# Attention keys on another DMA queue: stacks loaded in thirds, from a copy in DRAM that lies as in SBUF

## The chip, the cores and the metric

The kernel runs on one core of a Trainium2 chip. The metric is the device time of one execution in microseconds (us), as the median of several runs. A core has five engines that run side by side and wait for one another by semaphores: TensorE (PE, matrix products; PEld is its loading of weights), VectorE (DVE), ScalarE (ACT), GpSimd (POOL) and SyncE (SP), which here does nothing but issue DMAs. ScalarE can issue DMAs too; they then stand on a queue of its own, and among ScalarE's own instructions. SBUF is the core's memory with 128 partitions, PSUM the memory that TensorE writes, DRAM the large memory outside.

## What is computed

Four images of 384 channels and 48 x 48 = 2304 pixels pass through one attention layer with 8 heads of 48 channels. The queries get a depthwise 7 x 7 convolution of the image added.

```python
local = conv_general_dilated(x, conv_w, padding='SAME', feature_group_count=C)   # 7 x 7
local_flat = batch_norm(local).reshape(B, C, N).transpose(0, 2, 1)
x_norm = _layernorm(x_flat, ln_gamma, ln_beta)
q, k, v = (x_norm @ qkv_w.T + qkv_b)          # 8 heads of 48, N = 2304 pixels
q = q + _layernorm(local_flat, ln_gamma, ln_beta)
attn = softmax(einsum('bhnd,bhmd->bhnm', q, k) * scale)
out = einsum('bhnm,bhmd->bhnd', attn, v)
out = x_flat + (out @ proj_w.T + proj_b)
```

(The batch norm is written short here.) All tensors are float32.

## The kernel before

**Tiling.** An image's 2304 pixels are cut into NG = 6 groups of G = 384. There are NT = 24 groups over the four images, counted by t; b is the image and g the group in it. The 8 heads are worked in NP = 4 pairs. The keys' pixels are cut into KB = 18 blocks of 128.

**The attention of one group.** The loop from L1063 goes through NSLOT = 12 slots: 4 pairs, each in three thirds of BATCH = 6 key blocks. One slot is `score_batch` (L879) and `weigh_batch` (L884). `score` makes, for one key block, six matmuls of the stacked keys `ks` with the stacked queries `qs` (L856) into a PSUM tile `r`, and ScalarE takes the exponential of it (L864) into `pt`. `weigh_batch` multiplies the six `pt` of a slot with the values (L871) into a PSUM tile `o`, which ScalarE copies out (`sums_out`, L756 and L766) and VectorE adds up (`sums_add`, L775). Tiles `r` and `o` come from one pool of four buffers of two banks each.

**Stacks.** Scores are made at full float32 accuracy out of high and low parts. `key` (L570) splits the keys into a high part (L575, ScalarE) and a low part (L576, VectorE) in one tile `k` of 128 partitions x 2 x 384. `keys_out` (L519) writes `k` to the DRAM tensor `keys[b]`, head by head: four DMAs for each of the three tiles `k` of a group, since heads 6 and 7 are spread over all three. `stack_keys` (L533) then puts together the stack of a pair in SBUF: `stacks[b, p]`, 128 partitions x 2 x 2304, with high and low parts of two heads in the order that the six matmuls want. That takes eight DMAs: per head one of 48 partitions, one of 16 and two of 32. Two buffers hold stacks. For the first pair of an image's first group the stack is made piece by piece, a group's keys at a time; for all other pairs it is loaded whole, in the first third of the pair before (L1066 to L1070), so 23 whole stacks an image, each from `keys[b]`. Queries are stacked alike: `high_queries` (L725) casts on ScalarE (L728), `low_queries` (L730) subtracts on VectorE (L733) and then issues six DMAs (four for the last pair) that move rows of the tile within SBUF (L738, L740).

**Other small DMAs.** `sums_add` sends the softmax denominators `den` to DRAM (L780), and after the last pair moves rows of the outputs (`ao`, L784). `divide` (L788) loads them again as `rd` (L794), inverts them on VectorE (L795), writes them (`rden`, L799) and spreads them over partitions (`rb`, L804 and L807). The layer norms' sums go over DRAM as `parts` and `four` (L460, L461), and `few_in` reads `four` on VectorE (L470). `gather_tails` (L509) collects the fourth pair's queries in `qt` (L513) after `query_end` (L714). `load_slab` brings image rows for the convolution, `load_x` the next image's x (both L94), `hold` and `fetch` outputs that wait for their projection.

**The rest.** Between images the loop from L1009 makes keys, values and queries of the next image, and projects the last image's outputs. The convolution (L288) is 147 VectorE operations a group; a planner (`plan`, L358) spreads them over the slots. In the groups whose `coming` is true, the next image's x is loaded and normalised as well: the last two groups of the first image and the last three of the second and third.

**Order.** Instructions on TensorE, VectorE and ScalarE stand as the program writes them (`manual_schedule`, L84). All DMAs named so far are SyncE's, and their order on SyncE is the framework's. A DMA waits at issue for its data, for its buffer, and for one of eight completion semaphores that the framework gives out in turn.

Of the kernel before, what the change touches and what calls it, by code (L numbers as in the profile page):

```python
# [10 lines left out]
F32 = mybir.dt.float32  # L11
HALF = mybir.dt.float32r
# [4 lines left out]
P = 128  # L17
NH = 8
HD = 48
# [5 lines left out]
BATCH = 6  # L25
# [20 lines left out]
def unshifted_pass(  # L46
# [16 lines left out]
    nc = tc.nc  # L63
    B, C, N = x.shape
# [3 lines left out]
    G = RG * W  # L68
    NG = N // G
    NB = G // P  # L70
    NP = NH // 2
# [7 lines left out]
    big = ctx.enter_context(tc.tile_pool(name="big", bufs=1))  # L79
    work = ctx.enter_context(tc.tile_pool(name="work", bufs=2))  # L80
    dram = ctx.enter_context(tc.tile_pool(name="dram", bufs=2, space=bass.MemoryType.DRAM))
# [4 lines left out]
    def two_banks(name="r"):  # L86
        return ps.tile([P, 2, 512], F32, tag="r", name=name)
# [15 lines left out]
    def load_x(b, g):  # L103
        load_packed(place_x(b, g), x[b, :, g * G : (g + 1) * G])
# [79 lines left out]
    for c in range(CC):  # L184
        for r, n, first in ((0, HD, 0), (64, HD, 1), (48, 16, 6), (112, 16, 7)):
            head = first + 2 * c if first < 6 else first
            ch = head * HD + (16 * c if first >= 6 else 0)
            while n:
                part = min(n, P - ch % P)
                pieces.append((c, r, ch // P, ch % P, part))  # L190
                r, n, ch = r + part, n - part, ch + part
# [141 lines left out]
    def later(b):  # L333

        return X_LATER + (b == 1)
# [33 lines left out]
    def convolve(*point):  # L369
        for _ in range(share[point]):  # L370
            next(stream)
# [145 lines left out]
    keys, values = {}, {}  # L517

    def keys_out(b, g, u, k):  # L519
        at = slice(g * G, (g + 1) * G)  # L520
        for j in range(2):
            r = 64 * j
            for head, rows, n in (
                (2 * u + j, slice(0, HD), (r, r + HD)),
                (6 + j, slice(16 * u, 16 * u + 16), (r + HD, r + 64)),
            ):
                nc.sync.dma_start(
                    out=keys[b][head, rows, :, at], in_=k[n[0] : n[1]].bitcast(F32)
                )

    stacks = {}

    def stack_keys(b, p, at=slice(0, N)):  # L533

        if at.start == 0:
            stacks[b, p] = big.tile([P, 2, N], HALF, tag="ks", name=f"ks{b}_{p}", bufs=2)
        dst = stacks[b, p].bitcast(F32)
        for j in range(2):
            r, head = 64 * j, keys[b][2 * p + j]
            nc.sync.dma_start(out=dst[r : r + HD, 0, at], in_=head[:, 0, at])  # L540
            nc.sync.dma_start(out=dst[r + HD : r + 64, 0, at], in_=head[0:16, 1, at])
            for i in range(2):
                nc.sync.dma_start(
                    out=dst[r + 32 * i : r + 32 * i + 32, 1, at], in_=head[16:HD, 1, at]
                )

    def from_x(b, g, before=None, ao=None):

# [63 lines left out]
    def both(making):  # L612
        next(making)
        next(making)
# [7 lines left out]
    rows = {}  # L622
# [64 lines left out]
    def output_bias():  # L687

        m = two_banks()[:, 0, 0:CC]
        for co in range(CC):  # L690
            project(
                m[:, co : co + 1],
                lambda c: w_o[:, c, co * P : (co + 1) * P],
                lambda c: vbp[:, c, :],
            )
        added = const.tile([P, CC], F32, tag="inv", name="added")
        nc.scalar.copy(added, m)
        return added
# [4 lines left out]
    def local_end(t, rs):  # L703
        acc = accs[t]
        nc.vector.scalar_tensor_tensor(acc, acc, -1.0, rs, ALU.mult, ALU.mult)
# [19 lines left out]
    def high_queries(t, p):  # L725
        qs = work.tile([P, 3, G], HALF, tag="qs", name=f"qs{t}_{p}", bufs=5)
        stacked[t, p] = qs
        nc.scalar.copy(qs[:, 0, :], query_of(t, p))  # L728
# [39 lines left out]
    def sums_add():  # L768

        if not parts_of:  # L770
            return
        t, p, i, part = parts_of.popleft()
        ao, ao3, den = outputs[t]
        dst = (ao[:, p, :] if p < CC else ao3)[0 : 64 + HA]
        nc.vector.tensor_add(dst, dst, part[0 : 64 + HA])  # L775
        if i < KB // BATCH - 1:
            return
        for j in range(2):
            r = 64 * j
            nc.sync.dma_start(out=den[2 * p + j : 2 * p + j + 1], in_=dst[r + HD : r + HA])  # L780
        if p == NP - 1:
            for c in range(CC):
                for r in (0, 64):
                    nc.sync.dma_start(  # L784
                        out=ao[r + HD : r + 64, c, :], in_=ao3[r + 16 * c : r + 16 * c + 16]
                    )
# [25 lines left out]
    def load_residual(t, tag="qs", bufs=5):  # L812
        b, g = divmod(t, NG)
        xr = work.tile([P, CC, G], F32, tag=tag, name=f"xr{t}", bufs=bufs)
        nc.sync.dma_start(
            out=xr, in_=x[b, :, g * G : (g + 1) * G].rearrange("(c p) n -> p c n", p=P)
        )
        residuals[t] = xr
# [81 lines left out]
    def convolve_first(n):  # L900
        nonlocal n_first
        n_first += n
        for _ in range(n):
            next(stream)
# [58 lines left out]
    convolve_first(4)  # L963
    norm.scale(norm.newton())
    both(making)
    stack_keys(0, 0, slice(0, G))
    convolve_first(7)
    for g in range(1, NG):

        last = g == NG - 1  # L970
        making = from_x(0, g)
        both(making)
        assert not last or n_first >= each - PE_TAPS
        norm = Norm(accs[0] if last else xn[0, g + 1])
        norm.sum()
        norm.mean()
        if last:
            added = output_bias()
        convolve_first(4)
        norm.centre()  # L980
        norm.squares()
        both(making)
        if not last:
            convolve_first(4)
            both(making)
        norm.sum_squares()
        norm.mean()
        norm.root()
        if last:
            both(making)  # L990
        both(making)
        convolve_first(6 if last else 10)
        if last:
            local_end(0, norm.newton())
        else:
            norm.scale(norm.newton())
        both(making)
        stack_keys(0, 0, slice(g * G, (g + 1) * G))
        if not last:
            convolve_first(7)  # L1000
    query_end(0)
# [5 lines left out]
    for t in range(NT):  # L1007
        b, g = divmod(t, NG)
        if g == 0 and b:  # L1009

            sums_add()
            load_x(b, NG - 1)
            norms_x = {}
            for gk in range(NG):
                before = t - NG + gk
                load_residual(before)
                making = from_x(b, gk, before, ao if gk < NG - 1 else outputs[before][0])
                new = NG - later(b) + gk if gk < later(b) else None
                old = norms_x.get(gk - 1)
                both(making)  # L1020
                convolve("kv", t, gk, 0)
                if new is not None:
                    norms_x[gk] = Norm(xn[b, new])
                    norms_x[gk].sum()
                    norms_x[gk].out()
                both(making)
                if old:
                    old.few_variance()
                    old.few_root()
                if gk == 1:  # L1030
                    query_end(t)
                    rb = divide(t - 1)
                if gk == 2:
                    last_ao = outputs[t - 1][0]
                    nc.vector.tensor_mul(last_ao, last_ao, rb)
                convolve("kv", t, gk, 1)
                both(making)
                convolve("kv", t, gk, 2)
                if new is not None:
                    norms_x[gk].few_centre()  # L1040
                    norms_x[gk].squares()
                both(making)
                convolve("kv", t, gk, 3)
                if old:
                    old.scale(old.few_newton())
                both(making)
                convolve("kv", t, gk, 4)
                if new is not None:
                    norms_x[gk].sum_squares()
                    norms_x[gk].out()  # L1050
                both(making)
                stack_keys(b, 0, slice(gk * G, (gk + 1) * G))
                if gk == NG - 2:
                    high_queries(t, 0)
                if gk == NG - 1:
                    low_queries(t, 0)
                if gk < NG - 2:
                    ao = fetch(before + 1)
# [4 lines left out]
        for s in range(NSLOT):  # L1063
            score_batch(t, s)
            pair, third = divmod(s, KB // BATCH)
            if third == 0:  # L1066
                if pair < NP - 1:
                    stack_keys(b, pair + 1)
                elif g < NG - 1:
                    stack_keys(b, 0)  # L1070
            if third == 1 and pair < NP - 1:
                high_queries(t, pair + 1)
            if s == 2 and g:
# [71 lines left out]
    for before in range(NT - NG, NT):  # L1145
# [3 lines left out]
        r, r2 = two_banks(), two_banks()  # L1149
# [552 lines left out]
```

## Time and profile before

| | us |
|---|---|
| median of 3 runs | 3101.54 |
| lowest and highest | 3089.67, 3103.32 |
| the profiled execution | 3096.22 |
| its span, first to last instruction | 3094.4 |
| start-up until the first scores | about 190 |
| one group of the attention | 88 to 113 |
| from one image's attention to the next one's | 162 to 175 |

The profile shows one execution. "Busy" is time in which an engine works; a wait is put down to what ended last before the instruction began ("releaser"). "PEclk" is the share of TensorE's full clock that was granted; over the span it was 0.957. DMA issues are not counted as busy, but the timeline shows them, on "SPq" for SyncE and "ACTq" for ScalarE. Over the span the DMA engines moved 401 MB, at a share of 0.64 of their time, nearly all of it from SyncE's queue. In the section on DMA issues the stacks are the three largest entries: 184 DMAs of 432 KB, 368 of 288 KB and 184 of 144 KB.

### The profile page before, as it was taken

The page shows a single profiled execution, that of the slowest core. Times are in us where ns is not written, and L with a number is a line of the kernel's source. Part 1 is how long each engine was busy: PE and PEld are TensorE (multiplying, and loading weights), DVE is VectorE, ACT ScalarE, POOL GpSimd, SP SyncE. Part 2 cuts the span into 40 slices and gives each one's busy share as a digit, 9 for nine tenths or more (in the row PEclk, how much of TensorE's full clock was granted, in tenths as well). Part 3 has the DMA queues.
Part 4 walks back from the last instruction along what each step waited for, and adds up shares of the span by engine and source line. Part 5 has one row for each costly group of instructions (what it writes and reads, how often), then busy time and mean ns, then how long its engine had stood idle before and what let it go on. Part 6 is the DMA issues. An engine that isn't in the chain of part 4 may idle for free.

```text
span 3094.4 us, 52948 instructions
## 1 busy us (share of the span) xinstructions
PE 2846.5 (92%) x19190; PEld 1786.4 (58%) x19190; DVE 2474.7 (80%) x4899; ACT 1655.1 (53%) x2638; POOL 14.9 (0%) x77
## 2 busy tenths in 40 slices
PE   8877898889988999898999899999999989999999
PEld 5445555555555666565655566555555556656665
DVE  7779889888889788786789888878878877888612
ACT  4245555556522666665642366656663246666663
POOL 1000000000000000000000000000000000000000
PEclk9888999999998999999999999999999999999999
DMA  6255666777645767767654677677675557767774
GB/s 135 61 106 97 125 114 126 131 130 132 134 118 144 127 129 134 133 128 137 131 133 129 145 131 137 128 133 134 125 144 129 152 113 138 133 131 143 133 143 157
DMA packets 190926, 401.08 MB, mean 130 GB/s; under 512 B 69504, under 2 KB 150848, under 8 KB 167104
## 3 DMA queue, kind: packets, MB, share of 16 engines
q1 hardware_dynamic: 187120, 393.98, 64.1%
q8 instruction: 154, 2.52, 0.4%
q10 hardware_dynamic: 2992, 3.62, 0.3%
q14 instruction: 116, 0.95, 0.1%
q0 software_dynamic: 544, 0.01, 0.0%
HBM read 307.88 MB, written 55.35 MB: 117 GB/s over the span
## 4 chain that ended last, share of the span: by engine, by line
PE 34%; DVE 33%; DMA 22%; SPq 7%; issue 2%; ACT 1%; POOL 0%; DVEq 0%; ACTq 0%; POOLq 0%
DVE acc L288 21%; PE r L507 13%; PE o L871 11%; PE r L856 10%; DMA ks<-keys 7%; DMA four<-parts 4%; DMA xn<-in_x_dram 3%; DMA parts<-part 3%; SPq L740 3%; DMA qs<-qs 2%; SPq L738 1%; DVE sq L405 1%; DMA rd<-den 1%; DMA rden<-rd 1%; DVE sq L456 1%
## 5 line engine op out<-in xcount | busy, mean ns | idle before, releaser
L288 DVE SCALAR_TENSOR_TENSOR acc<-slab,vec,acc 128x368 f32<-128x368 f32 (+6 forms) x3447 | 1768.5, 587 | 1.2
L864 ACT ACTIVATE pt<-r 128x768 f32<-128x768 f32 x1728 | 1259.7, 827 | 337.6 <-PE r L856 298.9
L856 PE MATMUL r<-qs,ks 64*128 64x384 f32 x10368 | 1092.9, 357 | 201.6 <-DMA qs<-qs 118.3
L856 PEld LDWEIGHTS r<-qs,ks 64*128 64x128 f32 x10368 | 955.3, 196 | 418.7 <-issue 265.9
L871 PE MATMUL o<-pt,v 128*64 128x384 f32 x6912 | 1183.6, 492 | 0.0
L871 PEld LDWEIGHTS o<-pt,v 128*64 128x64 f32 x6912 | 472.8, 137 | 593.0 <-issue 510.6
L507 PE MATMUL r<-xn,w_qk 128*128 128x384 f32 x864 | 293.1, 498 | 0.0
L756 ACT COPY o<-o 113x384 f32<-113x384 f32 x192 | 91.7, 478 | 320.8 <-PE o L871 320.7
L507 PEld LDWEIGHTS r<-xn,w_qk 128*128 128x128 f32 x864 | 169.7, 196 | 120.7 <-issue 11.8
L795 DVE RECIPROCAL rd<-rd 128x24 f32<-128x24 f32 x24 | 7.3, 303 | 189.3 <-DMA rd<-den 189.3
L507 PE MATMUL r<-w_v,xn 128*128 128x384 f32 x432 | 147.0, 493 | 9.7 <-DVE xn L502 8.9
L567 ACT COPY v<-r 128x384 f32<-128x384 f32 x72 | 32.1, 480 | 187.7 <-PE r L507 187.7
L507 PEld LDWEIGHTS r<-w_v,xn 128*128 128x128 f32 x432 | 82.2, 192 | 69.9 <-DVE xn L502 10.5
L470 DVE TENSOR_REDUCE few<-four 128x12 f32<-128x48 f32 x80 | 18.6, 233 | 129.7 <-DMA four<-parts 129.7
L766 ACT COPY ao<-o 113x384 f32<-113x384 f32 x72 | 34.6, 481 | 163.8 <-PE o L871 163.8
L507 PE MATMUL r<-af,w_o 128*128 128x384 f32 x360 | 119.1, 487 | 0.0
L733 DVE TENSOR_TENSOR qs<-xn,qs 128x384 fp32r<-128x384 f32 x72 | 40.0, 556 | 95.9 <-ACT qs L728 95.9
L576 DVE SCALAR_TENSOR_TENSOR k<-r,qkb,k 128x384 fp32r<-128x384 f32 x72 | 44.4, 616 | 67.8 <-ACT k L575 67.4
L507 PEld LDWEIGHTS r<-af,w_o 128*128 128x128 f32 x360 | 68.3, 190 | 47.7 <-issue 0.6
L775 DVE TENSOR_TENSOR ao<-ao,o 113x384 f32<-113x384 f32 x144 | 79.7, 554 | 18.2 <-ACT o L756 18.2
L575 ACT ACTIVATE k<-r,qkb 128x384 fp32r<-128x384 f32 x72 | 41.9, 582 | 92.4 <-PE r L507 43.3
L588 ACT ACTIVATE xn<-r,qkb 128x384 f32<-128x384 f32 x72 | 39.4, 576 | 57.6 <-PE r L507 56.3
(119 smaller groups left out, 906.2 us busy)
## 6 DMA issues: line engine op xcount, KB each, us to landing
ks<-keys SPq DMA_DIRECT2D x368, 288.0 KB
ks<-keys SPq DMA_DIRECT2D x184, 432.0 KB
ks<-keys SPq DMA_DIRECT2D x184, 144.0 KB
qs<-qs SPq DMA_DIRECT2D x528, 48.0 KB
keys<-k SPq DMA_DIRECT2D x144, 144.0 KB
xr<-in_x_dram SPq DMA_DIRECT2D x24, 576.0 KB
slab<-in_x_dram SPq DMA_DIRECT2D x32, 378.0 KB
held<-ao SPq DMA_DIRECT2D x20, 576.0 KB
```

The costliest lines, as they stand in the source:

```text
L288: nc.vector.scalar_tensor_tensor(dst, src, weight, dst, ALU.mult, ALU.add)
L507: nc.tensor.matmul(dst, lhsT=weights(c), rhs=src(c), start=c == 0, stop=c == CC - 1)
L575: nc.scalar.activation(k[:, 0, :], r[:, :G], AF.Identity, bias=bias)
L576: nc.vector.scalar_tensor_tensor(k[:, 1, :], r[:, :G], bias, k[:, 0, :], ALU.add, ALU.subtract)
L588: nc.scalar.activation(src[:, i, :], q[:, :G], AF.Identity, bias=qkb[:, 0, i : i + 1])
L733: nc.vector.tensor_sub(qs[:, 1, :], query_of(t, p), qs[:, 0, :])
L740: nc.sync.dma_start(out=qs[r + 32 * i : r + 32 * i + 32, 2], in_=qs[r + 16 : r + HD, i])
L756: nc.scalar.copy(part[0 : 64 + HA], sums[0 : 64 + HA, 0, :G])
L775: nc.vector.tensor_add(dst, dst, part[0 : 64 + HA])
L856: nc.tensor.matmul(r[:, j, :G], lhsT=ks[rows, w, kb * P : (kb + 1) * P], rhs=qs[rows, m, :], start=i == 0, stop=i == 2,)
L864: nc.scalar.activation(pt, r[:, :, :G], AF.Exp, scale=SCALE)
L871: nc.tensor.matmul(sums[halves[j], 0, :G], lhsT=values[t // NG, kb // NB][:, first : first + 64], rhs=pt[:, j, :], start=i == 0, stop=i == ...
```

## The change

Four things change; the instructions of TensorE, VectorE and GpSimd stay in their order.

- **Whole stacks come on ScalarE's queue.** `stack_keys` goes. `load_keys` (b, p, i) is called in every third of a pair, after the scores of that slot, for the next pair.
- **From a copy, in thirds.** In the second third of each pair of an image's first group, `keep_stack` writes the stack to DRAM as it lies in SBUF (`wide`, 128 x 2 x 2304), in one DMA of 2.36 MB. From the second group on, `load_keys` brings one third of a stack (128 x 2 x 768) in one DMA per slot.
- **In the first group** the copy doesn't exist yet for pairs 1 to 3; these are loaded whole, with eight DMAs from `keys[b]`, on ScalarE's queue. Pair 0 of the second group is already loaded from the copy.
- **The first pair is stacked straight from SBUF.** When `key` has made the first of a group's three tiles (u = 0, which holds heads 0 and 1), `keys_out` issues eight DMAs from it into the stack, and no longer writes these heads to `keys[b]`.

```diff
     def keys_out(b, g, u, k):
         at = slice(g * G, (g + 1) * G)
+        k = k.bitcast(F32)
+        if u == 0:
+            if g == 0:
+                place_keys(b, 0)
+            for j in range(2):
+                stack_head(b, 0, j, k[64 * j : 64 * j + HD], at, nc.sync)
         for j in range(2):
             r = 64 * j
...
+            if u:
+                nc.sync.dma_start(out=keys[b][2 * u + j, :, :, at], in_=k[r : r + HD])
+            nc.sync.dma_start(
+                out=keys[b][6 + j, 16 * u : 16 * u + 16, :, at], in_=k[r + HD : r + 64]
+            )
...
+    def stack_head(b, p, j, head, at, queue):
+
+        dst, r = stacks[b, p].bitcast(F32), 64 * j
+        queue.dma_start(out=dst[r : r + HD, 0, at], in_=head[:, 0])
+        queue.dma_start(out=dst[r + HD : r + 64, 0, at], in_=head[0:16, 1])
+        for i in range(2):
+            queue.dma_start(out=dst[r + 32 * i : r + 32 * i + 32, 1, at], in_=head[16:HD, 1])
+
+    def keep_stack(b, p):
+        wide[b, p] = dram.tile([P, 2, N], F32, tag=f"wide{p}", name=f"wide{b}_{p}")
+        nc.scalar.dma_start(out=wide[b, p], in_=stacks[b, p].bitcast(F32))
+
+    def load_keys(b, p, i):
+        if i == 0:
+            place_keys(b, p)
+        if (b, p) in wide:
+            at = slice(i * BATCH * P, (i + 1) * BATCH * P)
+            nc.scalar.dma_start(
+                out=stacks[b, p].bitcast(F32)[:, :, at], in_=wide[b, p][:, :, at]
+            )
+        elif i == 0:
+            for j in range(2):
+                stack_head(b, p, j, keys[b][2 * p + j], slice(0, N), nc.scalar)
...
             score_batch(t, s)
             pair, third = divmod(s, KB // BATCH)
-            if third == 0:
-                if pair < NP - 1:
-                    stack_keys(b, pair + 1)
-                elif g < NG - 1:
-                    stack_keys(b, 0)
+            if g == 0 and third == 1:
+                keep_stack(b, pair)
+            if pair < NP - 1 or g < NG - 1:
+                load_keys(b, (pair + 1) % NP, third)
```

The three calls of `stack_keys(b, 0, ...)` at the ends of the key stages (L966, L998, L1052) are gone. The changed kernel is 13 lines longer; lines from L531 on move by up to 17.

More of the change, by code (lines that the diff above doesn't have):

```diff
@@ L520, in keys_out @@
         at = slice(g * G, (g + 1) * G)
+        k = k.bitcast(F32)
[4 more added lines that the diff above has]
+                stack_head(b, 0, j, k[64 * j : 64 * j + HD], at, nc.sync)
         for j in range(2):
             r = 64 * j
[L523 to L545, printed above, removed]
+            if u:
+                nc.sync.dma_start(out=keys[b][2 * u + j, :, :, at], in_=k[r : r + HD])
@@ new lines, in keys_out, with place_keys @@
+            nc.sync.dma_start(
+                out=keys[b][6 + j, 16 * u : 16 * u + 16, :, at], in_=k[r + HD : r + 64]
+            )
+    stacks, wide = {}, {}
+    def place_keys(b, p):
+        stacks[b, p] = big.tile([P, 2, N], HALF, tag="ks", name=f"ks{b}_{p}", bufs=2)
+    def stack_head(b, p, j, head, at, queue):
[4 more added lines that the diff above has]
+            queue.dma_start(out=dst[r + 32 * i : r + 32 * i + 32, 1, at], in_=head[16:HD, 1])
@@ L965, in unshifted_pass @@
     both(making)
-    stack_keys(0, 0, slice(0, G))
     convolve_first(7)
@@ L997, in unshifted_pass @@
         both(making)
-        stack_keys(0, 0, slice(g * G, (g + 1) * G))
         if not last:
@@ L1051, in unshifted_pass @@
                 both(making)
-                stack_keys(b, 0, slice(gk * G, (gk + 1) * G))
                 if gk == NG - 2:
```

## The prediction

> **What bounds the kernel now.** I read the page first, for shares. Columns of its groups: busy time, mean ns of one, idle time before it and what ended most of that.
>
> ```profile
> PE 2846.5 (92%) x19190; PEld 1786.4 (58%) x19190; DVE 2474.7 (80%) x4899; ACT 1655.1 (53%) x2638; POOL 14.9 (0%) x77
> ...
> L864 ACT ACTIVATE pt<-r 128x768 f32<-128x768 f32 x1728 | 1259.7, 827 | 337.6 <-PE r L856 298.9
> L856 PE MATMUL r<-qs,ks 64*128 64x384 f32 x10368 | 1092.9, 357 | 201.6 <-DMA qs<-qs 118.3
> ...
> L795 DVE RECIPROCAL rd<-rd 128x24 f32<-128x24 f32 x24 | 7.3, 303 | 189.3 <-DMA rd<-den 189.3
> ```
>
> TensorE is the bound. Its scores wait for the queries' DMAs, and VectorE waits 189 us for one small DMA that comes 24 times. Next the table by stretch (length, then busy time of PE, PEld, DVE, ACT, POOL; clock; DMA share; GB/s), three groups of twelve slots:
>
> ```profile
> 1189.00:1285.00 96.00, 92.86 (x721) 59.39 (x721) 84.49 (x165) 61.88 (x94) 0.00 (x0) 0.96 0.70 129
> 1285.00:1391.00 106.00, 95.62 (x724) 60.06 (x724) 85.57 (x175) 63.17 (x100) 0.00 (x0) 0.95 0.69 131
> ...
> 2874.00:2962.00 88.00, 86.38 (x697) 56.88 (x699) 48.57 (x102) 59.42 (x91) 0.00 (x0) 0.98 0.77 139
> ```
>
> The last shows the floor: 88 us. The middle one, which also normalises the next image's x, takes 18 more, 10 as idle TensorE and most of the rest as a lower clock. Why, the timeline of the SyncE queue, then TensorE and ScalarE, shows (start, length, what; idle before in brackets):
>
> ```profile
> 1291.06 0.30 SPq L541 DMA_DIRECT2D ks<-keys  x1
> 1292.83 0.96 SPq L543 DMA_DIRECT2D ks<-keys  x2
> 1296.50 3.97 SPq L94 DMA_DIRECT2D xn<-in_x_dram  x4
> 1303.20 1.06 SPq L780 DMA_DIRECT2D den<-aot  x2
> 1305.49 5.75 SPq L784 DMA_DIRECT2D ao<-aot  x6
> 1311.34 0.53 SPq L738 DMA_DIRECT2D qs<-qs  x1
> ```
>
> ```profile
> 1305.09 4.09 PE L871 MATMUL o<-pt,v 128*64 128x384 f32 x24
> 1313.55 0.66 PE L856 MATMUL r<-qs,ks 64*128 64x384 f32 x1 [4.37 <-DMA qs<-qs]
> 1315.45 5.77 PE L856 MATMUL r<-qs,ks 64*128 64x384 f32 x35 [1.24 <-DMA qs<-qs]
> ```
>
> ```profile
> 1302.64 4.33 ACT L864 ACTIVATE pt<-r 128x768 f32<-128x768 f32 x6 [0.29 <-PE r L856]
> 1309.22 0.48 ACT L756 COPY o<-o 113x384 f32<-113x384 f32 x1 [2.26 <-PE o L871]
> ```
>
> VectorE had finished the sums at 1292.1 and the low queries at 1302.75; their DMAs were issued at 1303.2 and 1311.3. They stood in SyncE's order behind the stack. The reason is in SyncE's waits (total, times, longest):
>
> ```profile
> SPq L780 <- DMA ks<-keys: 112.6, 78, 3.0
> SPq L784 <- DMA ks<-keys: 87.7, 80, 2.7
> ```
>
> A `den` or `ao` needs nothing of a stack. In the built program eight completion semaphores go round over all hardware DMAs, and each DMA waits at issue for the last user of its own. After eight stack DMAs, the next must wait for them to land. The ScalarE lines matter for the other side: after six exponentials ScalarE idles 2.26 us until TensorE has the next sum.
>
> [...] No trace of before shows two busy queues (q1 has 64.1% of the engines' time, all others below 1%). [...] 36 score matmuls took 3.41 us before the stall and 6.4 after it.
>
> **The change, part by part.**
>
> Removed from SyncE: 23 stacks of 8 DMAs per image, 736 issues of about 0.42 us, and what waited on their semaphores.
>
> (a) Groups that load the next image's x: five full ones last 106 to 107 us, their neighbours without it 94 to 97: 10 more each, and three shorter last groups I put at 4. 5 x 10 + 3 x 4 = 62. The stall above (5.6 us, and 3 of half clock) is over half of one such 10; the rest is a later VectorE (it waited 14.27 us for rd, 3.75 for four), which the same queue caused. I take 80%: 50.
> (b) Second to fourth group of the first image: 107, 108 and 105 us at VectorE busy 92 to 99. Its wait for rd (5.7 in one) shrinks; VectorE bounds the gain: 6 each, 18.
> (c) Start of images two to four: TensorE waits 11.7, 11.3 and 10.0 us for queries whose DMAs stood about 4 us behind the last piece of the stack. The first pair is now stacked from SBUF with the group's first keys, ahead of them: 3 x 3.7 = 11.
> (d) Eight groups without x: their starts wait 1 to 4 us, partly queue: 1.5 each, 12.
> Gain 91.
>
> Added on ScalarE, behind the six exponentials of a slot, with the copy of the sum, the cast of the next queries and the next exponentials behind it. Price of an issue: the 18 output DMAs on ScalarE took 0.34 each, SyncE's stack DMAs 0.42; one per slot lies in the 2.26. TensorE feels a hold only beyond 2.26 plus about 0.3 (its tiles come round four deep). So the cost is the waits for semaphores, from the built program, with the trace's time for what they wait for:
>
> (e) First group of each image. Eight DMAs at once in slots 0, 3, 6: 2.7 to 3.8 us, up to 1.3 too long; 3 x 1 x 4 = 12. In slot 6 they also wait for the copy kept two slots before (2.36 MB at the 200 GB/s which 130 at a share of 0.64 means: 12 us, and as much x as comes between) and, in images one and three, for VectorE's sums or a slab: 3 to 7 each, 18 in all. Images one and three wait for a slab in slot 7 too, and image one for its own first DMA in slot 3: 8. Sum 38.
> (f) Slot 10. The load waits for the first piece of `qt` (L513), which VectorE releases at L714; it lands 1.9 us later. The cast needs only L714. So cast and sum copy come 1.9 + 0.4 later: in sixteen groups 0.3 to 2.3, some 20, half of it inside the wait at the next group's start, which ends by VectorE: 10.
> (g) In some 30 loads the semaphore is that of the load one slot (7.36 us) before. A third is 0.79 MB: 4 us and 2 to land, 5 more beside a slab. Mostly hidden: 6. Slot 0 waits for den: VectorE's sum comes 0 to 2.4 us after the exponentials, plus 2.6: over the slack in two groups, 3.
> Loss 57.
>
> (h) Copies to DRAM: 16 x 2.36 MB = 38 MB on 401; the engines stand at 0.64. No cost but in (e). Bounds: 0 to 10.
>
> Not shown by this trace: a wait held on ScalarE. Bounds for (e) to (g): 25 (issues alone) and 140 (every wait as late as the old queue made its DMA). For (a) to (d): 50 (only stalls whose queries were ready) and 125 (all of them and the half clock). I take 57 and 91: net -34.
>
> Order on TensorE, VectorE and GpSimd is unchanged. Projections, weights and convolution cost nothing new.
>
> **Sum.** The profiled run took 3096.2 (span 3094.4); 3096 - 34 = 3062. The median of the runs is 5 higher, 3101.5, so 3067 for a median.
>
> **Rivals.**
> 1. The queue is relieved and ScalarE mostly hides its waits (forecast): 3067, own range 3030 to 3084. For it: 2.26 us idle in nearly all slots.
> 2. ScalarE's holds win. Place: slots 0, 3, 6, 7 of first groups and slot 10 of all. Price: 140, and gains of only 60, for VectorE's work then starts late too: 3101 + 80 = 3181 at worst; typically 100 against 65: 3136. It decides when holds beyond 2.5 us exceed some 90 us in sum, that is when slot 10 is not absorbed and first groups lose over 15 each. For it: [...] those semaphores. Against: the DMAs they belong to land earlier once the stacks are elsewhere.
> 3. The wait stays where it was. Six query DMAs at 0.62 and 2 to land already take 5.1 us after L733; many starts in the trace show just that. Then the gain is 45, the loss 50: 3106, within 0.5%. Against: the seven pair starts like that at 1309, where the low queries were ready 6 to 9 us before.
> 4. Better: VectorE, free of its DMA waits, removes all stalls: 125 against 40: 3016. For it: 189 and 130 us of waits for rd and four. Against: VectorE is 80% busy.
>
> **How the numbers follow.** Chances: first 0.40, second 0.30, third 0.20, fourth 0.10. A measurement of this kernel tells about 0.5% (15 us) from no change. The first gives 0.36 faster and 0.04 same; the second 0.27 slower and 0.03 same; the third 0.13 same, 0.05 slower and 0.02 faster; the fourth 0.10 faster. Faster 0.48, same 0.20, slower 0.32. Range: 3005 to 3140; it leaves out half of the second and a little of the fourth.
>
> **What would show it.** Right: no `SPq <- DMA ks` waits, DVE's wait for rd under 60 us, PE's for qs under 70, groups with x near 97, `ACT pt L881` still ended by PE. Wrong: PE waits ended by ACT's sum copy (L773, L783), with ScalarE idle until a DMA; first groups of images over 115 us; a mean clock under 0.957.

## The result, and the profile after

| | before | after |
|---|---|---|
| median of four runs, us | 3097.22 (3089.67 to 3103.32) | 3058.65 (3047.61 to 3064.02) |
| ratio, 95% interval | | 0.9872 [0.9834, 0.991] |
| profiled execution, us | 3096.22 | 3060.85 |
| its span, us; granted clock | 3094.4; 0.957 | 3059.1; 0.959 |

The changed kernel is 1.3% faster, some 40 us. Ratios, here and below, compare fast runs; a single run, of 5599.69 us with the whole loads of experiment 4, fell into a slower state and counts only in that kernel's median. The page of after: busy times, the two DMA queues (packets, MB, share of 16 engines), then groups.

```profile
PE 2832.8 (93%) x19190; PEld 1788.7 (58%) x19190; DVE 2475.5 (81%) x4899; ACT 1655.3 (54%) x2638; POOL 14.9 (0%) x77
...
q10 hardware_dynamic: 75184, 258.44, 28.6%
q1 hardware_dynamic: 146416, 169.80, 22.3%
...
L881 ACT ACTIVATE pt<-r 128x768 f32<-128x768 f32 x1728 | 1261.2, 826 | 307.3 <-PE r L873 266.4
L873 PE MATMUL r<-qs,ks 64*128 64x384 f32 x10368 | 1077.3, 356 | 189.0 <-DMA qs<-qs 103.5
...
L750 DVE TENSOR_TENSOR qs<-xn,qs 128x384 fp32r<-128x384 f32 x72 | 40.0, 556 | 217.9 <-ACT qs L745 217.9
```

Work is what it was. TensorE's idle time before scores is hardly smaller (189 after 201.6), though two queues now share what one did. One thing stands out: the two queues together move more (428 MB after 394 on q1 alone) in less of the engines' time (50.9% after 64.1%). The waits on all engines (total, times, longest), then SyncE's own:

```profile
PE r L873 <- DMA qs<-qs: 103.5, 47, 8.4
DVE few L470 <- DMA four<-parts: 91.3, 31, 9.8
...
DVE rd L812 <- DMA rd<-den: 1.0, 1, 1.0
```

```profile
SPq L757 <- ACT qs L745: 397.7, 63, 12.6
...
SPq L757 <- DMA ks<-keys: 143.4, 28, 13.6
```

VectorE's wait for `rd` is gone (189.3 to 1.0), TensorE's for the queries is not. SyncE's DMAs now wait for ScalarE's cast of the queries (397.7 us on a line that waited 27.6 for it before), and 28 times still for a stack's DMA, now one on the other queue. By stretch (length, busy PE, PEld, DVE, ACT, POOL, clock, DMA share, GB/s): the second image's first group, one without the next x and one with it:

```profile
967.00:1083.00 116.00, 99.58 (x720) 65.64 (x720) 84.82 (x166) 62.67 (x94) 0.00 (x0) 0.90 0.73 185
1176.00:1267.00 91.00, 88.75 (x724) 56.75 (x720) 85.03 (x167) 61.24 (x94) 0.00 (x0) 1.00 0.48 141
1361.00:1455.00 94.00, 89.77 (x720) 56.34 (x719) 81.26 (x170) 62.39 (x100) 0.00 (x0) 1.00 0.56 148
```

Full groups went from 95 or 106 us to 91 and 94; the first group of an image went from 95.5 to 116. Over all groups (length from one group's first score to the next one's, read from the trace) the full ones and those at an image's end give back about 123 us, the four first groups take 84 (482.6 after 399.0), start and end 4.5: that leaves 35, the difference of the two profiled executions. What a first group looks like, third image, ScalarE and then TensorE:

```profile
1774.24 0.31 ACTq L543 DMA_DIRECT2D ks<-keys  x1
1774.59 0.43 ACTq L544 DMA_DIRECT2D ks<-keys  x1
1775.06 1.33 ACTq L546 DMA_DIRECT2D ks<-keys  x2
1781.13 0.31 ACTq L543 DMA_DIRECT2D ks<-keys  x1
1787.01 0.31 ACTq L544 DMA_DIRECT2D ks<-keys  x1
1789.60 0.91 ACTq L546 DMA_DIRECT2D ks<-keys  x2
1790.55 0.48 ACT L783 COPY ao<-o 113x384 f32<-113x384 f32 x1 [15.57 <-DMA slab<-in_x_dram]
```

```profile
1791.08 3.25 PE L873 MATMUL r<-qs,ks 64*128 64x384 f32 x18 [12.01 <-ACT ao L783]
```

From 1775 to 1790.5 ScalarE does nothing but issue the DMAs of one stack, and wait at them, the last time for a slab's load; TensorE stands 12 us for a copy of 0.48 us.

### The profile page after: what moved, and what is told of

It is laid out like the page before. It is cut to its first block, busy times and chain, and to the rows that moved or that the text cites. A ratio compares the mean times of both kernels' runs of the same rounds, so it can differ in the third digit from the quotient of the medians.

```text
span 3059.1 us, 52436 instructions
## 1 busy us (share of the span) xinstructions
PE 2832.8 (93%) x19190; PEld 1788.7 (58%) x19190; DVE 2475.5 (81%) x4899; ACT 1655.3 (54%) x2638; POOL 14.9 (0%) x77
## 4 chain that ended last, share of the span: by engine, by line
PE 51%; DVE 25%; DMA 17%; ACT 2%; SPq 2%; issue 2%; ACTq 1%; DVEq 0%
PE r L873 19%; PE o L888 19%; DVE acc L288 15%; PE r L507 12%; DMA qs<-qs 6%; DMA qt<-xn 3%; DMA ks<-keys 3%; DMA parts<-part 2%; DMA four<-parts 2%; DVE xn L731 1%; ACT pt L881 1%; DVE acc L722 1%; DMA slab<-in_x_dram 1%; DVE sq L405 1%; DVE sq L404 1%
## 5 line engine op out<-in xcount | busy, mean ns | idle before, releaser
L873 PE MATMUL r<-qs,ks 64*128 64x384 f32 x10368 | 1077.3, 356 | 189.0 <-DMA qs<-qs 103.5
L750 DVE TENSOR_TENSOR qs<-qt,qs 128x384 fp32r<-128x384 f32 x24 | 13.3, 556 | 70.3 <-ACT qs L745 70.3
```

The costliest lines, as they stand in the source:

```text
L750: nc.vector.tensor_sub(qs[:, 1, :], query_of(t, p), qs[:, 0, :])
L873: nc.tensor.matmul(r[:, j, :G], lhsT=ks[rows, w, kb * P : (kb + 1) * P], rhs=qs[rows, m, :], start=i == 0, stop=i == 2,)
```

## The experiments

Ratios are to the kernel before, run beside each on the same chip. Three questions: what ScalarE's queue costs, what the gain is made of, and how the queue costs it.

**1. The same loads, issued by SyncE step by step.** First only the whole loads of first groups, then the copies too, then the thirds as well.

```diff
-                stack_head(b, p, j, keys[b][2 * p + j], slice(0, N), nc.scalar)
+                stack_head(b, p, j, keys[b][2 * p + j], slice(0, N), nc.sync)
```

> The changed kernel, but the eight whole loads of each image's first group are issued by SyncE; copies and thirds stay on ScalarE. Theory A (the change gains about 128 us from SyncE's freed queue and loses about 84 in the four first groups because ScalarE is held at issue of these loads): the first groups, 126, 116, 125 and 115 us in the changed kernel, come down to 96 to 102, what remains is the copy's own hold; time 2985 to 3010. Theory B (first groups are slow because 2.36 MB are written to DRAM while the next stack comes in, whoever issues): first groups stay above 110, time 3040 to 3060.

```diff
-        nc.scalar.dma_start(out=wide[b, p], in_=stacks[b, p].bitcast(F32))
+        nc.sync.dma_start(out=wide[b, p], in_=stacks[b, p].bitcast(F32))
```

> As the run before, and the copies to DRAM are issued by SyncE too; ScalarE issues the thirds alone. Theory A: first groups 95 to 98, time 2975 to 2995, a little below the run before if the copy held ScalarE in slots 4, 7 and 10. Theory B: as the run before, 3040 to 3060; and the queries' DMAs, again behind 2.36 MB on one queue, make TensorE wait in slots 3, 6 and 9 of the first groups.

```diff
-            nc.scalar.dma_start(
+            nc.sync.dma_start(
                 out=stacks[b, p].bitcast(F32)[:, :, at], in_=wide[b, p][:, :, at]
             )
```

> The changed kernel with every load and copy of stacks issued by SyncE, nothing on ScalarE: one DMA per third instead of eight per stack, but the old queue. Theory A (the queue matters: small DMAs stand behind stacks): half or more of the gain outside the first groups is lost, groups with the next image's x at 98 to 104, time 3030 to 3075. Rival C (the gain is from fewer DMAs: with one DMA per slot the eight completion semaphores are no longer all taken by one stack, the second queue adds nothing): groups with x stay at 93 to 96, time 2970 to 2995.

| all stack DMAs on ScalarE but | median, us | ratio, 95% interval | four first groups, us |
|---|---|---|---|
| none (after) | 3058.65 | 0.9872 [0.9834, 0.991] | 482.6 |
| first loads | 3014.92 | 0.9742 [0.972, 0.9765] | 431.6 |
| first loads, copies | 2985.65 | 0.9646 [0.9625, 0.9667] | 405.7 |
| first loads, copies, thirds | 2912.12 | 0.9406 [0.9383, 0.9429] | 403.4 |

Each step off ScalarE gains: 0.0130, 0.0096 and 0.0240, which at 3100 us are 40, 30 and 74. The first two times come out near what theory A had (the first 5 us above its range); the third is faster than either of its expectations. With nothing on ScalarE's queue the changed loads bring 5.9%. So the second queue brought none of the gain; it took 144 of 184 us away. The last kernel's page and stretches (same three groups):

```profile
q1 hardware_dynamic: 218608, 424.62, 52.2%
...
L873 PE MATMUL r<-qs,ks 64*128 64x384 f32 x10368 | 1028.0, 346 | 92.2 <-DMA qs<-qs 38.2
```

```profile
942.00:1035.00 93.00, 91.03 (x720) 58.45 (x720) 79.06 (x154) 61.03 (x93) 0.00 (x0) 0.97 0.86 222
1125.00:1213.00 88.00, 88.00 (x722) 56.59 (x720) 84.91 (x167) 61.09 (x94) 0.00 (x0) 1.00 0.49 146
1302.00:1392.00 90.00, 89.45 (x725) 56.93 (x721) 81.88 (x170) 62.91 (x100) 0.00 (x0) 1.00 0.55 155
```

On one queue, with 31 MB more than before, TensorE waits half as long, and the groups stand at the floor of 88 us. It isn't that SyncE had too much on it.

**2. A second queue on an engine that has nothing to lose.** All stack loads and copies on GpSimd.

```diff
-            nc.scalar.dma_start(
+            nc.gpsimd.dma_start(
```

> The changed kernel with all its stack loads and copies issued by GpSimd, which has nearly nothing else to do (15 us of work): a second queue whose waits at issue hold no engine that computes. If a second queue is worth something once its holds cost nothing, it beats the run with everything on SyncE (2912): 2880 to 2905. If the gain is all in the form of the loads, 2905 to 2925. If GpSimd's way of issuing makes the loads late, 2940 or more, with TensorE waiting for ks.

3188.57 us, ratio 1.0277 [1.0253, 1.0301]: as late as the last expectation allows with its "or more", but not for its reason, a wait for `ks`. TensorE waits for the queries, and SyncE for its small DMAs:

```profile
PE r L873 <- DMA qs<-qs: 182.7, 54, 9.1
```

```profile
SPq L461 <- DMA parts<-part: 295.6, 63, 16.4
```

No busy engine was held here, so a hold on ScalarE can't be all that a second queue costs.

**3. Parts of the change alone.** First the kernel before with only the first pair stacked from SBUF, as an edit of the changed kernel (heads 0 and 1 are still written to `keys` too, the stacks come from there, on SyncE):

```diff
-            if u:
+            if True:
...
-            if g == 0 and third == 1:
-                keep_stack(b, pair)
```

> The kernel before with one part alone: the first pair of each image's first group is stacked straight from SBUF; all other stacks come whole from keys[b] on SyncE as before. The prediction's step (c): image starts wait 3.7 us less for three images, 11 us in all, time 3083 to 3093, ratio about 0.9965. Rival: the eight SBUF to SBUF DMAs hold the tiles of the keys longer and the stages between images grow by what is gained; 3094 to 3100.

3100.32 us, 1.0012 [1.0002, 1.0023]: no gain, as the rival expectation had it. Then the other part: before, with the copy and its thirds on SyncE, and the first pair still through DRAM (shown is the call; `keep_stack` and `load_keys` are those of the change, with every DMA on SyncE).

```diff
-            if third == 0:
-                if pair < NP - 1:
-                    stack_keys(b, pair + 1)
-                elif g < NG - 1:
-                    stack_keys(b, 0)
+            if g == 0 and third == 1:
+                keep_stack(b, pair)
+            if pair < NP - 1 or g < NG - 1:
+                load_keys(b, (pair + 1) % NP, third)
```

> The kernel before with the copy and its thirds on SyncE, and the first pair still through DRAM as before: what the copy is worth without the stacking from SBUF. The latter was worth nothing by itself (3100 us). If the parts add up, 2912 to 2925. If the stacking from SBUF is worth my step (c) only once the queue is relieved, about 10 to 25 more at the starts of images two to four: 2925 to 2940.

2922.28 us, 0.9435 [0.9404, 0.9466], whose interval overlaps the 0.9406 that both parts bring. The loads from the copy are the whole gain; the stacking from SBUF can't be told from nothing in either place.

**4. Thirds, or few DMAs?** With everything on SyncE, the copy read back whole:

```diff
+            if i == 0:
+                nc.sync.dma_start(out=stacks[b, p].bitcast(F32), in_=wide[b, p])
```

> All on SyncE as in the run with everything on SyncE (2912 us), but a stack that has a copy comes in one whole DMA in the pair's first slot instead of three thirds. If the gain is from the number of DMAs (eight semaphores taken by a stack before, one now), 2895 to 2925. If the gain is from spreading the bytes over three slots, so that a query's DMA never stands behind a whole stack's bytes, a good part of it goes: 2950 to 3010, and TensorE's wait for qs grows from 38 us to 70 or more.

2950.58 us, 0.9509 [0.9474, 0.9545]: between the two expectations, with a wait for `qs` of 45.1 us rather than 70. Most of the gain is there without thirds; against one whole load thirds are worth 0.0103, or 32 us. The other way, the eight DMAs from the keys spread over the three slots as three, three and two, the first pair stacked from SBUF:

```diff
+            some = (((0, 1, 2), (3,), ()), ((), (0, 1), (2, 3)))[j][i]
+            stack_head(b, p, j, keys[b][2 * p + j], slice(0, N), nc.sync, some)
```

> The same eight DMAs per stack from the keys as before, on SyncE, no copy, but three, three and two of them in the pair's three slots instead of eight in the first (first pair stacked straight from SBUF as in the run that did this alone, 3100 us). If bunching of the eight was the cost, most of the gain of the run with everything on SyncE appears: 2920 to 2990. If the form of the DMAs (32 rows and 16 rows each, their descriptors and the time of the DMA engines) is the cost, it stays at 3060 to 3110.

3199.14 us, 1.0321 [1.0297, 1.0344], slower than both expectations. It brought a wait of its own that I had not priced, so it decides little:

```profile
PE r L868 <- DMA ks<-keys: 162.0, 63, 5.6
```

A stack's last two pieces, issued in the slot before they are needed, come too late.

**5. Eight DMAs from the copy, by rows or by columns.** Both with everything on SyncE and all eight in the pair's first slot, so the same data from the same place on the same eight semaphores (`dst` is the stack, `src` its copy). By rows they have the destinations of the old loads (48, 16, 32, 32 rows, twice); by columns each goes over all 128 partitions.

```diff
+            for r in (0, 64) if i == 0 else ():
+                nc.sync.dma_start(out=dst[r : r + HD, 0], in_=src[r : r + HD, 0])
+                nc.sync.dma_start(out=dst[r + HD : r + 64, 0], in_=src[r + HD : r + 64, 0])
+                for h in (r, r + 32):
+                    nc.sync.dma_start(out=dst[h : h + 32, 1], in_=src[h : h + 32, 1])
```

> As the run with one whole load (2950 us, first pair stacked from SBUF, everything on SyncE), but each stack is read from its copy by eight DMAs in the pair's first slot, with the very destinations of the loads from the keys: 48, 16, 32 and 32 rows of 9216 bytes, twice. If what made the loads from the keys dear is that there are eight of them, or that each writes few partitions, it goes back to 3070 to 3110, and packets of 9216 bytes take 750 to 850 ns as they did there. If it was where the data lies in DRAM (the keys against the copy), it stays at 2940 to 2970, with packets near 350 ns.

```diff
+            for h in range(2) if i == 0 else ():
+                for n in range(0, N, N // 4):
+                    nc.sync.dma_start(
+                        out=dst[:, h, n : n + N // 4], in_=src[:, h, n : n + N // 4]
+                    )
```

> Eight DMAs from the copy in the pair's first slot, like the run by rows, but each over all 128 partitions and a quarter of one half, 2304 bytes a row. If the number of DMAs counts (eight semaphores taken by one stack, eight issues of SyncE), 3050 to 3110, with the wait for rd back at 100 us or more. If the partitions that a DMA covers count, and so the DMA engines' time, 2930 to 2985, with packets of 2304 bytes near 100 ns and the wait for rd under 40 us.

By rows 3105.33 us, 1.0009 [0.9999, 1.0019]: the kernel before, in time and in its waits. By columns 2906.31, 0.9366 [0.9347, 0.9384]: all of the gain, and the lowest time of the kernels here, below what either theory gave. All eight go out in one slot, so the spreading over slots isn't what the thirds gained by. By rows, its page, waits, and SyncE's waits:

```profile
q1 hardware_dynamic: 184048, 424.65, 66.5%
```

```profile
DVE rd L814 <- DMA rd<-den: 180.8, 21, 16.7
...
PE r L875 <- DMA qs<-qs: 117.8, 93, 8.4
```

```profile
SPq L799 <- DMA ks<-wide: 95.8, 67, 3.3
SPq L803 <- DMA ks<-wide: 89.0, 79, 3.7
```

By columns:

```profile
q1 hardware_dynamic: 245488, 424.65, 52.7%
```

```profile
PE r L875 <- DMA qs<-qs: 45.6, 33, 8.5
...
DVE rd L814 <- DMA rd<-den: 6.9, 4, 3.2
```

```profile
SPq L803 <- DMA ks<-wide: 25.2, 65, 1.8
SPq L799 <- DMA ks<-wide: 19.1, 45, 1.1
```

The bytes are the same to the last digit. SyncE still waits for the stack's semaphores, 110 times after 146 on these lines, but for 44 us after 185, and VectorE's wait for `rd` is gone although eight DMAs still go out at once. Neither the number of DMAs nor the place in DRAM is the cause. The trace also has each packet of the DMA engines; those of the stacks:

```
loads of a stack                packet bytes   median ns   bytes per ns
before, from keys, by rows         9216           787          11.7
from the copy, by rows             9216           794          11.6
from the copy, by columns          2304            93          24.8
from the copy, thirds on SyncE     3072           121          25.4
from the copy, whole              18432           686          26.9
```

Over 128 partitions a packet moves at twice the rate (24.8 to 26.9 bytes a ns after 11.6 and 11.7), be it shorter or longer than 9216 bytes, so the packet's size isn't the reason either. Not varied by itself: loads of 16 to 48 rows also bring few packets at a time (16 to 48 a DMA, by columns 128). In the mean (828 ns, 256 packets, 16 engines) a stack took 13.2 us of all engines before, and takes 7.1 by columns (111 ns, 1024 packets). Nor do the loads by rows have one rate: in 30 stacks of before whose packets stand apart in the trace, those that by their order belong to a load of 16 rows took 981 and 1012 ns in the median, the 32 rows behind them 918 and 938, the last 32 of a head 712 and 722. The runs show that the partitions that a load covers count, or the packets that it brings at a time; what of them sets the rate was not shown.

**6. How the thirds on ScalarE cost 74 us.** The trace of the kernel with only the thirds on ScalarE, slot by slot against the one with none, puts 55 us into the first slot of groups. One such start there, its SyncE, ScalarE and TensorE:

```profile
2574.91 0.51 SPq L757 DMA_DIRECT2D qs<-qs  x1
2575.47 0.59 SPq L755 DMA_DIRECT2D qs<-qs  x1
2576.10 1.22 SPq L757 DMA_DIRECT2D qs<-qs  x2
```

```profile
2569.47 0.53 ACTq L557 DMA_DIRECT2D ks<-wide  x1
...
2575.69 0.53 ACTq L557 DMA_DIRECT2D ks<-wide  x1
```

```profile
2578.71 0.79 PE L873 MATMUL r<-qs,ks 64*128 64x384 f32 x5
2581.75 4.58 PE L873 MATMUL r<-qs,ks 64*128 64x384 f32 x31 [2.25 <-DMA qs<-qs]
```

And one with all on SyncE:

```profile
2514.97 1.22 SPq L757 DMA_DIRECT2D qs<-qs  x2
2516.28 0.58 SPq L557 DMA_DIRECT2D ks<-wide  x1
```

On SyncE the third of slot 11 stands behind the next group's queries; on ScalarE's queue it goes out beside them, and TensorE waits. Two runs tell this from ScalarE's being held. Both start from the kernel with only the thirds on ScalarE. In one the third of slot 11 goes to SyncE:

```diff
+            queue = nc.sync if (p, i) == (0, 2) else nc.scalar
```

> The run with only the thirds on ScalarE (2986 us), with one of them, that of a group's last slot, moved to SyncE, whose order puts it behind the next group's queries. The trace of that run shows 55 of its 73 us over the run with everything on SyncE in the first slot of a group. If the third's bytes beside the queries' DMAs cost them (their median landing in the first pair is 3.0 us with the thirds on ScalarE and 2.0 with all on SyncE), 2935 to 2960. If ScalarE's being held at the load of slot 10 cost them, nothing changes there: 2975 to 2990.

In the other that of slot 10, which waits at issue for `qt`, goes out a slot earlier:

```diff
-                load_keys(b, (pair + 1) % NP, third)
+                for i in ((0, 1), (), (2,))[third] if pair == NP - 1 else (third,):
+                    load_keys(b, (pair + 1) % NP, i)
```

> The run with only the thirds on ScalarE (2986 us), with the third of slot 10 issued in slot 9, ahead of the DMAs of qt on whose semaphore it waits. By my step (f) the holds at slot 10 cost 10 us: 2970 to 2980. If they are what lengthens the first slot of the next group by 55 us, 2930 to 2950. If neither, and the transfers beside the queries' DMAs cost it, 2978 to 2990.

The first gives 2940.14 us, 0.9472 [0.9451, 0.9493], the second 2980.64, 0.9611 [0.9576, 0.9645], against 0.9646 [0.9625, 0.9667]. Moving one third of twelve behind the queries returns 0.0174, or 54 us; ending the hold at slot 10 returns some 11, and the intervals overlap. The first slots of groups give back 59 us with the first edit and 4 with the second (the first edit loses some in other slots). TensorE's waits, with the thirds on ScalarE, with slot 11's moved, with slot 10's early:

```profile
PE r L873 <- DMA qs<-qs: 83.8, 38, 8.5
...
PE r L874 <- DMA qs<-qs: 52.1, 34, 8.5
...
PE r L873 <- DMA qs<-qs: 81.3, 34, 8.5
```

The landing of the queries for a group's first pair, from issue to the last completion of its semaphore, groups after an image's first, 120 DMAs each:

```
kernel                                   mean us   median us
before                                     2.03      1.96
after                                      3.55      3.13
thirds on ScalarE                          3.41      3.02
the same, slot 11's on SyncE               2.34      2.10
the same, slot 10's a slot earlier         3.57      3.63
all on SyncE                               2.34      2.02
all on GpSimd                              6.54      7.14
```

The last row explains part of the loss with GpSimd. Why GpSimd's transfers weigh so much more on the queries than ScalarE's is open; the trace shows its thirds in packets of 6144 bytes that take 247 ns in the median, where those from ScalarE have 3072 and take 121, and no run varied that alone.

## Why the prediction was right, and where it was not

The time was right (3067 predicted, 3058.65 measured) and so was the direction. That the number was met so closely is luck: it is the difference of two sums that were both far too small. By the runs, the new loads gained 184 us where 91 were predicted, and ScalarE's queue cost 144 where 57 were. Put beside the runs, the reasons fare worse than the sum. One reading of the trace of before was short as well. In the stall at 1309 the chain of waits (start, length) goes through the stack and then, for as long, through the loads of the next x:

```profile
1289.08 9.71 DMA ks<-keys
...
1298.81 11.24 DMA xn<-in_x_dram
```

- **Gains, (a), (b), (d).** In the groups of after 70 for 50, 21 for 18 and 22 for 12, with the thirds' cost still in them; with everything on SyncE 107, 26 and 43. The step that failed is the forecast's own ground, that the queue is relieved. That waits on a stack's semaphores delayed the small DMAs was right (experiment 5: they shrink from 185 us to 44 and the time goes with them), but in that stall it was half of the story. And I took the transfers' duration as given and the queue as what had to change. The loads' shape nearly halves the duration (13.2 us of all engines a stack, by columns 7.1): on the old queue that brings 184 us, and 0 with the new copy and the old shape. The copy, put at 12 us by the old rate, takes 5.9 of all engines in after with its packets' mean (735 ns), a third, put at 4, takes 2.5 (158 ns). Nor were 125 us a bound: I had taken it from the stalls and the half clock in groups (granted 0.50 from 1313.55 to 1316.00 of before) as I saw them, not from the floor of 88 us.
- **(c), starts of images.** The trace shows 10.0 us less stall there for the 11 predicted. But alone the edit took 8 us off the same stalls and nothing off the time (experiment 3): what the stall gives back is lost elsewhere, and where is open.
- **Losses, (e) and (h).** First groups lost 84, not 38. The mechanism was right, a DMA that waits on ScalarE holds the exponentials, but a hold lasted up to 15.57 us where I had allowed 3 to 7; the first loads cost 40. The copies, priced at nothing, cost 30 on ScalarE's queue. On SyncE's they cost next to nothing, though there the engines stand at 0.86 in the same group, for 0.73 in after: first groups take 403.4 us after 399.0. So the bytes had room, and the queue made the price; whether as holds or beside the queries is not separated.
- **(f), slot 10.** 10 predicted; 11 measured, with overlapping intervals and in the range that was given for no effect: not shown.
- **(g), the thirds.** This is the term that failed most: 9 predicted, and with (f) 74 measured. Its price was of holds. The larger part, 54, is bytes beside the next queries. How a small DMA fares beside a large one on another queue no trace of before showed, and I had given it no price; beside the thirds on ScalarE the queries landed 1.0 us later in the median (3.02 us, with all on SyncE 2.02), at the most critical place of a group.
- **Rivals.** What happened is the first rival's time, out of losses beyond the second's 140 (144) and gains beyond the fourth's 125 (184).
- **Signs.** Right: the wait for `rd` under 60 (1.0), groups with x near 97, exponentials still ended by TensorE. Missed: the wait for `qs` under 70 (103.5), and no waits of SyncE for stacks (143.4 on L757, from first groups). Of the signs of failure two appeared, first groups over 115 and TensorE waiting for ScalarE's copy (12.01), as an 84 us loss inside a gain.

## What to carry to other kernels

Look at how many partitions a DMA writes before looking at which queue it is on: here eight loads of 16 to 48 rows cost nearly twice the engine time of eight over 128 partitions (13.2 us a stack against 7.1), and that was 6% of the kernel. The second issuing engine took away order: large loads that the single queue kept behind small urgent ones ran beside them (54 us), and as ScalarE computes, its waits at issue held its work, up to 15.57 us at once. When a change does two things, put the new form on the old queue first.

## What the runs showed that I had not expected

- A packet of 9216 bytes to few rows takes 787 ns, one of 18432 bytes within a DMA over 128 partitions 686 ns.
- One whole load of 2.36 MB is 1.4% slower than eight over all partitions (0.9509 against 0.9366). Its packets occupy an engine for 0.69 us each instead of 0.09, and VectorE's wait for `four` is 141.9 us instead of 75.1; what of the difference comes from that was not separated.
- Loads issued by GpSimd, which is idle, made the kernel 2.8% slower than before, with the bytes and copy of the kernels that were 6% faster.
